# Reordering the candidate rows of a recurrent step and moving part of its operand preparation to GpSimd

## The chip, the cores and the metric

The kernel runs on one core of one Trainium2 chip. The metric is device time in microseconds (us), from one launch to its end; six runs of the kernel before gave a median of 1867.87 us (1865.36 to 1874.88). A profile of one execution goes with it. The engines of a core are named as the profile names them: PE (TensorE matrix multiply; PEld is its weight load), DVE (VectorE), ACT (ScalarE), POOL (GpSimd) and SP (SyncE, which here issues the DMAs). Each engine takes its own instructions strictly in the order in which the program has them, and waits on semaphores of others.

## The reference, cut to what matters

The input x has shape (4, 512, 512): batch B = 4, time T = 512, width D = 512. Four layers follow one another, each added to its input:

```python
x = x + attention(x, cond)               # 16 heads, RMS norm of q and k, all 512 keys
x = x + gru(cond, x)                     # one GRU over the 512 time steps
x = x + causal_conv(x, cond)             # 4 taps, depthwise
x = x + causal_conv(x, cond) + b         # 4 taps, depthwise
```

The GRU is the part that cannot be done in parallel over time. Its cell is:

```python
def cell(h, x):
    gi = x @ W_ih + b_ih
    gh = h @ W_hh + b_hh
    i_r, i_z, i_n = jnp.split(gi, 3, axis=-1)
    h_r, h_z, h_n = jnp.split(gh, 3, axis=-1)
    r = jax.nn.sigmoid(i_r + h_r)
    z = jax.nn.sigmoid(i_z + h_z)
    n = jnp.tanh(i_n + r * h_n)
    h_new = (1.0 - z) * n + z * h
    return (h_new, h_new)
```

## The kernel before, in words

A prologue of about 230 us loads and splits the weights, and computes keys, values and the first block. Then one loop over the 512 time steps runs the GRU (lines 1204 to 1272). All other work (attention, the products x @ W_ih and the convolutions, in 16 blocks of 32 time steps) is cut into small tasks that fill the gaps of the loop.

**One step of the loop.** The state h (4 batches of 512) is held as 128 partitions by 16 columns (k, b): k is one of four slices of 128 features, b the batch. It exists as an fp32 tile HS and an fp16 tile A; the kernel multiplies A by the low half of the weights (Wlo, fp16), and both A and the remainder HS - A by the high half (Whi), so that the product is good to about fp32. `prep` (line 1126) builds the operand tile BT for the next step, in eight slots of (k, b): DVE writes HS - A into slots 0 and 2 (line 1130), ACT writes A into the four odd slots (line 1131), and slots 4 and 6 stay zero. ACT also writes HH, half the state (line 1132). Then in each step

- PE adds to X (PSUM, r and z gates): 16 matmuls of A with Wlo, 16 of slots 0 and 1 of BT with Whi; and to Y (PSUM, n gate): 16 matmuls of slots 4 to 7 with Wlo and 16 of slots 0 to 3 with Whi (lines 1230 to 1239). The four column groups of PE each work on their own quarter of the features, and each quarter gives rows of 32 partitions, of which Y uses 16: slot by batch, four rows (batches) for each of four slots.
- DVE transposes X in blocks of 32 by 32 into TX (line 1241) and adds pairs into S (1243); ACT takes a tanh of it into ZT, the gates (1244).
- DVE transposes Y into TY (1253). The rows of Y come in the order slot, batch; the scan after it wants the four slots of each batch side by side, so the transposition writes with the batch innermost, at a step of four fp32 elements.
- DVE runs a scan over ZT and TY that sums the slots and multiplies by the gate (N, 1254), ACT takes the tanh (D1, 1255), DVE computes the other half of D1 from ZT and HH (1256), and two scans give the new A (1264) and HS (1265). PE waits for A and begins the next step.
- ACT also puts the next step's input products, G, into X (seedX, 1121) and Y (seedY, 1124), and POOL writes h + x into x2b for the convolutions (1269). G is loaded by SP, eight DMAs for every four steps (`load_g`, 1089), one step's four batches onto four neighbouring partitions of each group of 32.

**What sets the order.** The instruction order is fixed when the program is built. A small planner (class `Queue`) holds the tasks with priorities. Before the step's own matmuls, `q_.head` issues stages of tasks within a budget of modelled time for each engine (DVE 1130 ns, ACT 1900, POOL 3300); a single stage that costs more than the budget is let in if nothing of its engine has been issued in this step. After the step's own elementwise work, `q_.pe` issues matmuls of tasks for up to 1600 ns (2000 in the first 40 steps), and `keep_warm` adds a matmul on zeros where little was issued. Two steps before a new block of 32 steps begins (`t % 4 == GI_T`), `q_.flush` issues all that this block's input products still need, with no budget at all, ahead of the step's own matmuls. POOL's tasks are `nb` (line 447, one column, waits for DVE's row maximum `mx`), the convolution taps `tm` and `x` (lines 1168 and 1169, one pair a stage), and the Newton steps of an inverse square root for 14 of the blocks (lines 257 to 276, 13 POOL instructions, and 411 and 413; task R, line 421, one stage at a stated POOL cost of 4800).

**The end.** After the last step, the last block's convolution is issued at once: four ACT instructions (1153), then for each of six taps DVE does column groups 0 and 1 (1161), POOL groups 2 and 3; PE transposes the four groups (301), ACT copies, and SP stores.

Of the kernel before, what the change touches and what calls it, by code (L numbers as in the profile page):

```python
# [16 lines left out]
P = 128  # L17
# [145 lines left out]
def body(ctx, tc, x, cond, W_emb, b_emb, g_norm, W_qkv, g_q, g_k, W_out, W_ih, W_hh, b_ih, b_hh, L3_b, out):  # L163
# [24 lines left out]
    def rowmask(n, c):  # L188
        m = cst.tile([P, 1], F32, name=n)
        nc.vector.tensor_reduce(m, ident.rearrange("p (q s) -> p q s", q=4)[:, :, c], AX.XY, ALU.add)  # L190
        return m

    mr = mz = rowmask("mr", slice(0, 4))
    mh, mn = rowmask("mh", slice(4, 8)), rowmask("mn", slice(12, 16))

# [33 lines left out]
    BT = [cst.tile([P, 4, 8, 4], F16, name=f"BT{i}") for i in range(2)]  # L229
    for i in range(2):  # L230
        nc.gpsimd.memset(ZT[i], 1.0)
        nc.gpsimd.memset(ZT[i][:, :, :, 0:1], 0.0)
        nc.gpsimd.memset(D0[i], 0.0)
        nc.gpsimd.memset(BT[i], 0.0)
# [86 lines left out]
    def block_tasks(i):  # L321
# [72 lines left out]
        def rs0():  # L394
# [9 lines left out]
            if not pre_q:  # L404
                rsqrt(rq, v, 16, ear, nc.gpsimd)
                rs1()
# [13 lines left out]
        else:  # L420
            R = add(f"R{i}", deps=[Q], acq=["m", "L"], chunks=[(330, rch)], stages=[[("DVE", 410, rs0), ("Pool", 4800, lambda: None)]], rel=["m", "q"], settle=2)
# [638 lines left out]
    def scan_constants():  # L1060
# [4 lines left out]
        for v, m in ((sel, 1), (selY, 2)):  # L1065
            nc.gpsimd.memset(v, 0.0)
            nc.gpsimd.tensor_scalar(v[:, :, 4 * m:4 * m + 4], ident.rearrange("p (b t) -> p t b", b=4)[:, 0:2, :], 1.0, 1.0,
                                    ALU.mult, ALU.mult)

    sel, selY = lt("sel", [P, 2, 8]), lt("selY", [P, 2, 12])  # L1070
# [18 lines left out]
    def load_g(c):  # L1089
        g, i, t0_ = G[c % 2], c // 8, 4 * (c % 8)  # L1090
        for qq in range(4):
            nc.sync.dma_start(g[32 * qq + 4:32 * qq + 8, :, 0:2, :], GD[i][qq, :, t0_:t0_ + 4, 0:2, :])
            nc.sync.dma_start(g[32 * qq + 8:32 * qq + 12, :, 2, :], GD[i][qq, :, t0_:t0_ + 4, 2, :])  # L1093
# [3 lines left out]

    def dup(v):
        return v.rearrange("p (k b) -> p k b", k=4).unsqueeze(2).to_broadcast([P, 4, 2, 4])


    def seed_first(t, y):
# [12 lines left out]
        for qq in range(4 * y):  # L1115
            r = 32 * qq
            nc.tensor.matmul(Y[r:r + 12, :], selY[:, t], gs0["n"][:, qq, :], start=False, stop=True,
# [8 lines left out]
    def prep(A, HS, t):  # L1126

        Bt = BT[t % 2]
        HH = wk.tile([P, 16], F32, name="HH", tag="HH")
        nc.vector.tensor_tensor(Bt[:, :, 0:4:2, :], dup(HS[:, :, 1]), dup(A[:, :, 1]), ALU.subtract)  # L1130
        nc.scalar.activation(Bt[:, :, 1:8:2, :], A[:, :, 1].rearrange("p (k b) -> p k b", k=4).unsqueeze(2).to_broadcast([P, 4, 4, 4]), AF.Copy)  # L1131
        nc.scalar.activation(HH, HS[:, :, 1], AF.Copy, scale=0.5)
        return Bt, HH
# [11 lines left out]
    def conv_tasks(i):  # L1145
# [10 lines left out]
        def tap(k, jp):  # L1156
            def g():
                x4 = s["x4"].rearrange("p (a t) -> p a t", t=32)
                for j in (2 * jp, 2 * jp + 1):
# [139 lines left out]
```

## Time and profile before

| What | Value |
|---|---|
| median of 6 runs | 1867.87 us (1865.36 to 1874.88) |
| the profiled execution: its own time | 1867.61 us |
| its span, first to last instruction | 1865.7 us |
| PE busy | 1651.8 us, 89% |
| DVE busy | 1340.1 us, 72% |
| ACT busy | 1227.7 us, 66% |
| POOL busy | 451.6 us, 24% |
| first A of the loop to its last | 234.7 to 1846.2 us, 511 steps, 3.15 us each on average, 3.04 us median |
| after the last A | 19.5 us |
| granted TensorE clock | 0.985 |

The span is from the first to the last instruction; the execution's own time has 1.9 us around it. Busy shares are averages over stages and say little of a loop in which each engine waits for the next one: what counts in the loop is which wait ends last in a step. A line of the timeline reads: start, duration (both us), engine, source line, operation, tile written <- tiles read, and the number of instructions merged into it. A group's row ends in busy us and mean ns of one, then the engine's idle time before it and what ended it.

### The profile page before, as it was taken

The page shows a single profiled execution, that of the slowest core. Times are in us where ns is not written, and L with a number is a line of the kernel's source. Part 1 is how long each engine was busy: PE and PEld are TensorE (multiplying, and loading weights), DVE is VectorE, ACT ScalarE, POOL GpSimd, SP SyncE. Part 2 cuts the span into 40 slices and gives each one's busy share as a digit, 9 for nine tenths or more (in the row PEclk, how much of TensorE's full clock was granted, in tenths as well). Part 3 has the DMA queues.
Part 4 walks back from the last instruction along what each step waited for, and adds up shares of the span by engine and source line. Part 5 has one row for each costly group of instructions (what it writes and reads, how often), then busy time and mean ns, then how long its engine had stood idle before and what let it go on. Part 6 is the DMA issues. An engine that isn't in the chain of part 4 may idle for free.

```text
span 1865.7 us, 114008 instructions
## 1 busy us (share of the span) xinstructions
PE 1651.8 (89%) x48969; PEld 1174.9 (63%) x48969; DVE 1340.1 (72%) x4948; ACT 1227.7 (66%) x4701; POOL 451.6 (24%) x1480
## 2 busy tenths in 40 slices
PE   5789999999999999999999999999999998987553
PEld 2444567677667667676767676766667676765442
DVE  4785377776778687878777777777787877776664
ACT  4663375776767777767676767676767767665443
POOL 1255011322213131312222221313131312121212
PEclk9998899999999999999999999999999999999998
DMA  5662020101010102010101020100101010101000
GB/s 177 224 203 114 13 61 22 47 23 28 21 32 19 34 16 59 12 41 13 39 13 40 12 57 19 28 24 18 35 11 40 13 35 11 35 13 34 11 16 10
DMA packets 68921, 78.11 MB, mean 42 GB/s; under 512 B 6560, under 2 KB 54720, under 8 KB 67776
## 3 DMA queue, kind: packets, MB, share of 16 engines
q1 hardware_dynamic: 68416, 70.82, 12.6%
q8 instruction: 385, 6.31, 1.4%
q14 instruction: 120, 0.98, 0.2%
HBM read 44.58 MB, written 26.21 MB: 38 GB/s over the span
## 4 chain that ended last, share of the span: by engine, by line
PE 48%; DVE 25%; ACT 10%; DMA 6%; issue 6%; SPq 3%; POOL 1%; DVEq 0%; ACTq 0%; POOLq 0%
PE X L1227 21%; DVE TX L1241 5%; PE ps L439 5%; PE pgi L568 5%; PE Y L1227 5%; DVE TY L1253 5%; DMA G<-GD 5%; DVE N L1254 4%; PE ptp L301 4%; ACT D L1255 3%; DVE A L1264 3%; PE pkv L927 2%; PE po L483 2%; ACT X L1121 2%; SPq L1093 2%
## 5 line engine op out<-in xcount | busy, mean ns | idle before, releaser
L1227 PEld LDWEIGHTS <-BT 128*8 128x8 f16 (+1 forms) x24576 | 451.3, 88 | 81.6 <-issue 18.5
L1227 PE MATMUL X<-Wlo,A 128*4 128x256 f16 x8192 | 313.1, 272 | 125.4 <-DVE A L1264 89.1
L1244 ACT ACTIVATE ZT<-S 128x32 f32<-128x32 f32 x512 | 134.7, 263 | 415.7 <-DVE S L1243 415.1
L1269 POOL TENSOR_TENSOR x2b<-x,HS 128x16 f32<-128x16 f32 x512 | 126.8, 248 | 1130.0 <-DVE HS L1265 1128.7
L1241 DVE STREAM_TRANSPOSE TX<-X 128x256 f32<-128x256 f32 x512 | 229.4, 448 | 209.9 <-PE X L1227 208.5
L1227 PE MATMUL X<-Whi,BT 128*8 128x256 f16 x8192 | 315.7, 273 | 2.8 <-issue 2.6
L1227 PEld LDWEIGHTS <-A 128*4 128x4 f16 x8192 | 152.1, 83 | 217.6 <-DVE A L1264 191.6
L1253 DVE STREAM_TRANSPOSE TY<-Y 128x128 f32<-128x128 f32 x512 | 205.2, 401 | 10.6 <-PE Y L1227 4.3
L1227 PE MATMUL Y<-Whi,BT 128*16 128x128 f16 x8192 | 208.6, 219 | 4.7 <-issue 4.5
L1227 PE MATMUL Y<-Wlo,BT 128*16 128x128 f16 x8192 | 207.7, 219 | 4.4 <-issue 4.3
L1121 ACT ACTIVATE X<-G 128x256 f32<-128x256 f32 x510 | 202.3, 397 | 1.1 <-DMA G<-GD 0.4
L455 ACT ACTIVATE PX<-ps,nb,rqs 128x512 f32<-128x512 f32 x256 | 195.1, 762 | 8.7 <-POOL nb L447 4.7
L1254 DVE TENSOR_TENSOR_SCAN N<-ZT,TY 128x64 f32<-128x64 f32 x512 | 153.3, 299 | 54.7 <-ACT ZT L1244 2.1
L446 DVE TENSOR_REDUCE mx<-ps 128x1 f32<-128x512 f32 x256 | 174.8, 683 | 15.5 <-PE ps L439 15.4
L1264 DVE TENSOR_TENSOR_SCAN A<-D,D 128x32 f16<-128x32 f32 x512 | 115.3, 225 | 93.9 <-ACT D L1255 91.4
L301 PE MATMUL ptp<-ident,PX 128*128 128x128 f32 x1024 | 173.3, 291 | 1.0 <-ACT gs L576 0.6
L1131 ACT ACTIVATE BT<-A 128x64 f16<-128x64 f16 x512 | 131.2, 256 | 52.7 <-DVE A L1264 4.1
L301 PEld LDWEIGHTS ptp<-ident,PX 128*128 128x128 f32 x1024 | 111.4, 143 | 81.8 <-issue 43.7
L475 ACT ACTIVATE PT<-ptp 128x512 f32<-128x512 f32 x248 | 143.3, 582 | 15.1 <-PE ptp L301 15.1
L1124 ACT ACTIVATE Y<-G 128x128 f32<-128x128 f32 x510 | 141.5, 277 | 0.5 <-DMA G<-GD 0.5
L483 PEld LDWEIGHTS po<-V,PT 128*32 128x32 f32 x8192 | 99.0, 112 | 60.7 <-issue 51.8
L483 PE MATMUL po<-V,PT 128*32 128x32 f32 x8192 | 130.7, 200 | 5.8 <-issue 4.8
(266 smaller groups left out, 2806.6 us busy)
## 6 DMA issues: line engine op xcount, KB each, us to landing
GD<-gs SPq DMA_DIRECT2D x45, 256.0 KB
G<-GD SPq DMA_DIRECT2D x512, 16.0 KB
G<-GD SPq DMA_DIRECT2D x512, 8.0 KB
xp<-in_x_dram SPq DMA_DIRECT2D x16, 256.0 KB
xb<-in_x_dram SPq DMA_DIRECT2D x16, 256.0 KB
xhl<-XD SPq DMA_DIRECT2D x32, 128.0 KB
out_dram<-ob SPq DMA_DIRECT2D x16, 256.0 KB
wst<-in_L_cond_W_qkv_dram SPq DMA_DIRECT2D x6, 512.0 KB
```

The lines of the kernel that those rows point to most:

```text
L301: nc.tensor.transpose(dst[:, 128 * j:128 * j + 128], src[:, 128 * j:128 * j + 128], ident)
L446: nc.vector.tensor_reduce(s["mx"][:, h:h + 1], s[("s", j, q)], AX.X, ALU.max)
L455: nc.scalar.activation(pe_, s[("s", j, q)], AF.Exp, bias=s["nb"][:, h:h + 1], scale=s["rqs"][:, h:h + 1], accum_out=s["ls"][:, h:h + 1])
L475: nc.scalar.activation(pt_, s[("pt", h)], AF.Copy)
L483: nc.tensor.matmul(s["po"][32 * b:32 * b + 32, 32 * h:32 * h + 32], s["PT"][h][:, kt, 32 * b:32 * b + 32], V[:, 4 * b + kt, 32 * h:32 * h ...
L1121: nc.scalar.activation(X.rearrange("p (g c) -> p g c", g=2), G[(t // 4) % 2][:, t % 4, 0:2, :], AF.Copy)
L1124: nc.scalar.activation(Y, G[(t // 4) % 2][:, t % 4, 2, :], AF.Copy)
L1227: nc.tensor.matmul(dst[32 * qq:32 * qq + M, :], lhs, W[:, k, cols].rearrange("p g (j q s) -> p q g j s", j=4, q=4)[:, qq], start=False, st ...
L1241: nc.vector.transpose(TX.rearrange("p a r -> p (a r)"), X)
L1253: nc.vector.transpose(TY.rearrange("p h j b k -> p j h k b"), Y.rearrange("p (j h k b) -> p j h k b", j=4, h=2, k=4))
L1254: nc.vector.tensor_tensor_scan(f(NN), f(zt[:, 0]), TY[:, 0].rearrange("p j b k -> p (j b k)"), 0.0, ALU.mult, ALU.add)
L1264: nc.vector.tensor_tensor_scan(f(An), f(d0), f(D1), 0.0, ALU.mult, ALU.add)
```

## The change

Six things change together.

1. BT becomes two tiles. BX (k, 2 slots, b) serves X: DVE writes HS - A into slot 0 (16 columns instead of 32), ACT copies A into slot 1. BY (k, b, 4 slots) serves Y, with the slots innermost: POOL writes HS - A into slots 1 and 2, ACT copies A into slots 0 and 3. The low weights' 16 matmuls for Y now read all of BY too, so no zero slots remain and the rows of both products agree.
2. The rows of Y are so ordered by batch and then slot. The transposition into TY writes runs of 16 neighbouring elements. The seeds of Y, the masks for the biases and the DMAs into G follow: a G load for the n gate now goes to four partitions that lie four apart.
3. HH is computed by POOL, after BY and before x2b.
4. Task R has two stages, of stated POOL costs 1300 and 2000. The first issues the Newton steps up to the square of the second iteration, the second the rest and `rs1`.
5. In the last block, POOL keeps only column group 3, and DVE takes group 2 as well as 0 and 1.
6. The two memsets of BT go.

In the changed program's instruction order, the loop's waits follow: PE's first weight load from BX waits for DVE and ACT, the first from BY for ACT and POOL; DVE's part of D1 waits for POOL (HH); POOL's write of BY waits for DVE and PE.

```diff
@@ -188 +188 @@
-    def rowmask(n, c):
+    def rowmask(n, sel):
@@ -190 +190 @@
-        nc.vector.tensor_reduce(m, ident.rearrange("p (q s) -> p q s", q=4)[:, :, c], AX.XY, ALU.add)
+        nc.vector.tensor_reduce(m, sel(ident.rearrange("p (q b s) -> p q b s", q=4, b=8)), AX.XY, ALU.add)
@@ -193,2 +193,2 @@
-    mr = mz = rowmask("mr", slice(0, 4))
-    mh, mn = rowmask("mh", slice(4, 8)), rowmask("mn", slice(12, 16))
+    mr = mz = rowmask("mr", lambda v: v[:, :, 0, :])
+    mh, mn = rowmask("mh", lambda v: v[:, :, 0:4, 1]), rowmask("mn", lambda v: v[:, :, 0:4, 3])
@@ -229 +229,2 @@
-    BT = [cst.tile([P, 4, 8, 4], F16, name=f"BT{i}") for i in range(2)]
+    BX = [cst.tile([P, 4, 2, 4], F16, name=f"BX{i}") for i in range(2)]
+    BY = [cst.tile([P, 4, 4, 4], F16, name=f"BY{i}") for i in range(2)]
@@ -234 +234,0 @@
-        nc.gpsimd.memset(BT[i], 0.0)
@@ -405,2 +405,8 @@
-                rsqrt(rq, v, 16, ear, nc.gpsimd)
-                rs1()
+                s["nw"] = rsqrt_ops(rq, v, 16, ear, nc.gpsimd)
+                for _ in range(6):
+                    next(s["nw"])
+        def rs2():
+            for _ in s["nw"]:
+                pass
+            rs1()
@@ -421 +427 @@
-            R = add(f"R{i}", deps=[Q], acq=["m", "L"], chunks=[(330, rch)], stages=[[("DVE", 410, rs0), ("Pool", 4800, lambda: None)]], rel=["m", "q"], settle=2)
+            R = add(f"R{i}", deps=[Q], acq=["m", "L"], chunks=[(330, rch)], stages=[[("DVE", 410, rs0), ("Pool", 1300, lambda: None)], [("Pool", 2000, rs2)]], rel=["m", "q"], settle=1)
@@ -1065 +1071 @@
-        for v, m in ((sel, 1), (selY, 2)):
+        for v, c in ((sel, slice(4, 8)), (selY, slice(2, 16, 4))):
@@ -1067 +1073 @@
-            nc.gpsimd.tensor_scalar(v[:, :, 4 * m:4 * m + 4], ident.rearrange("p (b t) -> p t b", b=4)[:, 0:2, :], 1.0, 1.0,
+            nc.gpsimd.tensor_scalar(v[:, :, c], ident.rearrange("p (b t) -> p t b", b=4)[:, 0:2, :], 1.0, 1.0,
@@ -1070 +1076 @@
-    sel, selY = lt("sel", [P, 2, 8]), lt("selY", [P, 2, 12])
+    sel, selY = lt("sel", [P, 2, 8]), lt("selY", [P, 2, 16])
@@ -1093 +1099 @@
-            nc.sync.dma_start(g[32 * qq + 8:32 * qq + 12, :, 2, :], GD[i][qq, :, t0_:t0_ + 4, 2, :])
+            nc.sync.dma_start(g[32 * qq + 2:32 * qq + 18:4, :, 2, :], GD[i][qq, :, t0_:t0_ + 4, 2, :])
@@ -1097,4 +1102,0 @@
-    def dup(v):
-        return v.rearrange("p (k b) -> p k b", k=4).unsqueeze(2).to_broadcast([P, 4, 2, 4])
@@ -1117 +1119 @@
-            nc.tensor.matmul(Y[r:r + 12, :], selY[:, t], gs0["n"][:, qq, :], start=False, stop=True,
+            nc.tensor.matmul(Y[r:r + 16, :], selY[:, t], gs0["n"][:, qq, :], start=False, stop=True,
@@ -1128 +1130,7 @@
-        Bt = BT[t % 2]
+        Bx, By = BX[t % 2], BY[t % 2].rearrange("p k b s -> p (k b) s")
+        h4, a4 = (v[:, :, 1].rearrange("p (k b) -> p k b", k=4) for v in (HS, A))
+        two = lambda v: v[:, :, 1].unsqueeze(2).to_broadcast([P, 16, 2])
+        nc.vector.tensor_tensor(Bx[:, :, 0], h4, a4, ALU.subtract)
+        nc.gpsimd.tensor_tensor(By[:, :, 1:3], two(HS), two(A), ALU.subtract)
+        nc.scalar.activation(Bx[:, :, 1], a4, AF.Copy)
+        nc.scalar.activation(By[:, :, 0:4:3], two(A), AF.Copy)
@@ -1130,4 +1138,2 @@
-        nc.vector.tensor_tensor(Bt[:, :, 0:4:2, :], dup(HS[:, :, 1]), dup(A[:, :, 1]), ALU.subtract)
-        nc.scalar.activation(Bt[:, :, 1:8:2, :], A[:, :, 1].rearrange("p (k b) -> p k b", k=4).unsqueeze(2).to_broadcast([P, 4, 4, 4]), AF.Copy)
-        nc.scalar.activation(HH, HS[:, :, 1], AF.Copy, scale=0.5)
-        return Bt, HH
+        nc.gpsimd.tensor_scalar(HH, HS[:, :, 1], 0.5, 1.0, ALU.mult, ALU.mult)
+        return Bx, BY[t % 2], HH
@@ -1156 +1162 @@
-        def tap(k, jp):
+        def tap(k, jp, js=None):
@@ -1159 +1165 @@
-                for j in (2 * jp, 2 * jp + 1):
+                for j in js or (2 * jp, 2 * jp + 1):
@@ -1173,2 +1179,3 @@
-                  stages=[[("ACT", 700, lambda jp=jp: f1(jp))] for jp in range(2)] + [
-                      [("Pool", 900, tap_p(k, j))] + ([("DVE", 526, tap(k, 0))] if j == 2 else []) for k in range(1, 7) for j in (2, 3)],
+                  stages=[[("ACT", 700, lambda jp=jp: f1(jp))] for jp in range(2)] + ([
+                      [("Pool", 900, tap_p(k, j))] + ([("DVE", 526, tap(k, 0))] if j == 2 else []) for k in range(1, 7) for j in (2, 3)] if i < NB - 1 else [
+                      [("Pool", 900, tap_p(k, 3)), ("DVE", 526, tap(k, 0)), ("DVE", 300, tap(k, 1, (2,)))] for k in range(1, 7)]),
@@ -1202 +1209 @@
-        Bt, HH = prep(A, HS, 0)
+        Bx, By, HH = prep(A, HS, 0)
@@ -1233 +1240 @@
-                mm(X, Bt[:, k, 0:2, :].rearrange("p s b -> p (s b)"), 8, Whi, k, slice(0, 2))
+                mm(X, Bx[:, k].rearrange("p s b -> p (s b)"), 8, Whi, k, slice(0, 2))
@@ -1237 +1244 @@
-                mm(Y, Bt[:, k, 4:8].rearrange("p s b -> p (s b)"), 16, Wlo, k, slice(2, 3))
+                mm(Y, By[:, k].rearrange("p b s -> p (b s)"), 16, Wlo, k, slice(2, 3))
@@ -1239 +1246 @@
-                mm(Y, Bt[:, k, 0:4].rearrange("p s b -> p (s b)"), 16, Whi, k, slice(2, 3))
+                mm(Y, By[:, k].rearrange("p b s -> p (b s)"), 16, Whi, k, slice(2, 3))
@@ -1253 +1260 @@
-            nc.vector.transpose(TY.rearrange("p h j b k -> p j h k b"), Y.rearrange("p (j h k b) -> p j h k b", j=4, h=2, k=4))
+            nc.vector.transpose(TY.rearrange("p h j b k -> p j h (b k)"), Y.rearrange("p (j h r) -> p j h r", j=4, h=2))
@@ -1268 +1275 @@
-                Bt, HH = prep(A, HS, t + 1)
+                Bx, By, HH = prep(A, HS, t + 1)
```

## The prediction

> **What bounds the kernel now.** I read the page's chain of waits first, then the groups by line, then the timeline of single steps, and last the windows around the longest step.
>
> ```profile
> span 1865.7 us, 114008 instructions
> ...
> PE 48%; DVE 25%; ACT 10%; DMA 6%; issue 6%; SPq 3%; POOL 1%; DVEq 0%; ACTq 0%; POOLq 0%
> ...
> L1253 DVE STREAM_TRANSPOSE TY<-Y 128x128 f32<-128x128 f32 x512 | 205.2, 401 | 10.6 <-PE Y L1227 4.3
> ```
>
> No engine bounds the loop alone: the chain runs through PE, DVE and ACT in turn. One plain step, and the end of the step before it, in the timeline:
>
> ```profile
> 589.62 0.61 DVE L1161 SCALAR_TENSOR_TENSOR x<-x2b,VC,x 128x128 f32<-128x128 f32 x2
> 589.78 0.60 POOL L1168 TENSOR_SCALAR tm<-x2b,VC 128x128 f32<-128x128 f32 x1
> ...
> 592.39 0.22 DVE L1264 TENSOR_TENSOR_SCAN A<-D,D 128x32 f16<-128x32 f32 x1 [0.18 <-ACT D L1255]
> 592.53 0.20 DVE L1265 TENSOR_TENSOR_SCAN HS<-D,D 128x32 f32<-128x32 f32 x1
> ...
> 592.76 0.19 DVE L1130 TENSOR_TENSOR BT<-HS,A 128x32 f16<-128x32 f32 x1
> 592.81 0.25 POOL L1269 TENSOR_TENSOR x2b<-x,HS 128x16 f32<-128x16 f32 x1 [1.71 <-DVE HS L1265]
> ...
> 593.03 0.37 POOL L1168 TENSOR_SCALAR tm<-x2b,VC 128x128 f32<-128x128 f32 x1
> ...
> 593.48 0.46 POOL L1169 TENSOR_TENSOR x<-tm,x 128x128 f32<-128x128 f32 x1
> 593.54 0.40 PE L1227 MATMUL Y<-Wlo,BT 128*16 128x128 f16 x16
> ...
> 593.76 0.45 DVE L1241 STREAM_TRANSPOSE TX<-X 128x256 f32<-128x256 f32 x1 [0.21 <-PE X L1227]
> ...
> 594.25 0.19 DVE L1243 TENSOR_TENSOR S<-TX 128x32 f32<-128x32 f32 x1
> ...
> 594.36 0.40 DVE L1253 STREAM_TRANSPOSE TY<-Y 128x128 f32<-128x128 f32 x1
> 594.47 0.27 ACT L1244 ACTIVATE ZT<-S 128x32 f32<-128x32 f32 x1 [0.70 <-DVE S L1243]
> ...
> 594.86 0.30 DVE L1254 TENSOR_TENSOR_SCAN N<-ZT,TY 128x64 f32<-128x64 f32 x1
> 594.94 0.21 ACT L1247 ACTIVATE D<-ZT 128x16 f32<-128x16 f32 x1
> ...
> 595.19 0.18 ACT L1255 ACTIVATE D<-N 128x16 f32<-128x16 f32 x1
> ...
> 595.41 0.23 DVE L1264 TENSOR_TENSOR_SCAN A<-D,D 128x32 f16<-128x32 f32 x1 [0.18 <-ACT D L1255]
> ```
>
> The step is 3.02 us from A to A. PE starts 0.28 after A and its Y matmuls at 1.15; then TX, S, TY, N, the tanh D and A follow without a hole. N starts 0.10 after TY's end and 0.12 after ZT's. Over the 512 steps the first is 103 ns (102 to 104 in most), the second 124 ns in the median. In the 14 steps where ZT came late, N started 32 ns after ZT. So TY holds N, and ZT would hold it about 92 ns earlier.
>
> A second bound stands beside this chain: PE's filler. In 112 of 511 steps PE's first X matmul starts more than 60 ns after A's end (55 is the least): PE was still at other work.
>
> **The change, part by part.** Moments below count from a step's start at A. The sum is made against the profiled execution, 1867.61 us, 0.26 under the median.
>
> *TY (once a step).* A transposition of the same size, also from PSUM, that writes its columns in order:
>
> ```profile
> L397 DVE STREAM_TRANSPOSE rt<-pr x16: 305/308/310, 62.7 to 1489.9; 128x128 f32<-128x128 f32 x16
> ```
>
> TY takes 401 and steps four elements per write; the new one writes runs of 16. I take 308, so 93 ns less (bounds: 0, if a pattern of several dimensions is what costs, and 93). Next late is ZT, which allows 92, and then ACT: the tanh D follows the ACT instruction before it (L1247) by at least 119 ns, and here by 250, so it allows 130 in this step. Taking the least of the three in every step gives a mean of 79 ns. A step whose PE had no slack gains nothing, one with little slack gains that: summed over 511 steps this is 26 (by matmul durations) to 30 us (by PE's idle time before X). I take -27, bounds -22 to -30 where TY falls as said.
>
> *prep on DVE and ACT.* DVE's 32 columns (195 ns, L1130) become 16 (164, from the 16-column row L1256): 30 ns earlier for the filler behind it. ACT's 256 + 202 ns become two copies, near 202 each: HH leaves, and the filler behind starts no later. PE's first weight load from BX is wanted at 0.69 and BX is there by 0.57: 0.
>
> *BY on POOL (512 instructions).* It starts where x2b starts, 0.42, and costs between 0.25 (x2b, 16 columns) and 0.46 (L1169, 128 columns); 0.27 by the nearer row. It lands at 0.67 to 0.88, and PE's Y matmuls start at 1.15: 0. Behind it on POOL stand HH (0.20) and x2b, so all other POOL work begins 0.43 later. HH lands by 0.9, or 1.2 behind DVE's taps, against its reader at 2.65: 0. `nb` feeds an exponential of the next step: 0. PE gains a double wait at BY's first weight, with Y and the filler queued behind it: today's double wait between X's Wlo and Whi matmuls costs nothing (0.43 us from start to start, and 0.44 from Whi to Y, where nothing waits), so 0. BY's own wait for PE's reading two steps back is long met; D1's for HH has the scans A and HS behind it.
>
> The page "GPSIMD Engine Reference" of the Trainium skill, section Engine selection, speaks against this move: elementwise work with two inputs runs about half as fast there. By that rule an estimate for BY is 2 x 195 = 390 ns, landing at 0.81, still early, and the sum stays.
>
> *Meetings of DVE and POOL.* The first two lines of the timeline fence show one: beside DVE's two taps POOL's `tm` took 0.60, alone 0.37. The other way round, in 8 steps BT met POOL's `x` and took 338 ns instead of 192, ending 46 ns after it. With POOL 0.43 later, `x` reaches to 1.98 in a step without DVE taps (S runs 1.86 to 2.06 there: 46 ns after `x` is 2.03, so 0, up to 0.06 if BY is slower, in about 90 steps). In a step with DVE taps and `mx`, S runs 2.09 to 2.28 and `x` to 2.30, so S ends 0.06 later: 66 steps, +4 us. I take +5, bounds 0 and 12.
>
> The page "SBUF — State Buffer" of the Trainium skill, section Who interferes with whom, calls this an exclusive lock and would let each such pair wait out the other. The rows agree for `x` and the taps, not for x2b: it overlapped BT in every step and both kept their times. By the rule BY would begin only when DVE's subtraction ends, at 0.54, and land by 1.0, still ahead of 1.15.
>
> *Newton stages.* One POOL instruction follows another by 0.29 (steps after 595.4). The second stage has 9 behind x2b: to 1.11 + 2.65 = 3.76, where the next BY wants POOL at 3.37. That BY lands 0.4 late, near 1.10, against 1.15. 14 blocks: 0 to 1.4 us, I take 0.5.
>
> *What the planner makes of the new POOL costs.* 4800 shut POOL to all other tasks for a step, 1300 and 2000 do not, so tasks shift. In the program order of the changed kernel DVE's taps meet `mx` in 66 steps instead of 49: 17 x 0.23 (the step at 589.14 is 3.25 long against 3.02), less 30 ns of BX in some 70 late steps: +2 us (0 to 4). More weighty: before, one flush falls into the loop, at step 62:
>
> ```profile
> 434.50:443.40 8.90, 8.86 (x245) 7.08 (x244) 3.15 (x10) 4.35 (x15) 0.44 (x2) 1.00 0.17 45
> ```
>
> The columns are stretch, length, then busy time of PE, PEld, DVE, ACT and POOL. A to A it is 8.87, thus 5.85 more than a plain step, and PE is busy throughout. The changed order has that flush and two more, ahead of steps 190 and 350, with 35 `pgi`, 20 `ps`, 10 `ptp` and 48 `po` matmuls each, the same PE time within 5%. 2 x 5.85 = +11.7 (9 to 14). The work so brought forward no longer overfills other steps: -3.7, from PE time by step in both orders.
>
> *The G loads.* As many DMAs of the same size on SP's queue, to partitions four apart: their landing is not shown. They are issued three steps, 9 us, ahead of use, and ACT now waits 0.5 us for them in all: 0; a loss would need that cover gone.
>
> *The end.*
>
> ```profile
> 1846.58 5.21 DVE L1161 SCALAR_TENSOR_TENSOR x<-x2b,VC,x 128x128 f32<-128x128 f32 x12
> ...
> 1857.42 0.45 POOL L1169 TENSOR_TENSOR x<-tm,x 128x128 f32<-128x128 f32 x1
> ```
>
> POOL's 12 pairs, 0.92 each, end at 1857.87. Six end near 1852.4; DVE's 18 taps, 0.43 beside POOL and about 0.27 alone, end near 1853.5 and are last. -4 us (-3.3 to -4.4). Memsets and masks of the prologue: beside DMA waits, 0.
>
> Sum: -27 - 3.7 + 11.7 + 2 + 5 + 0.5 - 4 = -15.5, so 1852 for the profiled execution, 1852.4 against the median. With all ends at their best 1839, at their worst 1870.
>
> **The rivals.** (B) Slower: the shorter TY does not move N, because ZT's release costs as much as TY's does now (0.10 instead of 0.03), or TY stays at 401. For it: N has two waits, and the 32 ns come from 14 steps alone. Against it: those steps agree with every other release from ACT to DVE (D to A, 32 ns). With N unmoved the 27 are gone: 1880. With ZT at 0.10 the mean shift is 28 ns, worth 11: 1869. It decides the sign when the loop gains less than 11.5, about 34 ns a step. (C) Meetings and flushes cost their upper bounds, POOL's later queue holding S: 1853 + 7 + 2.3 = 1862. For it: POOL's busy time nearly doubles, 452 us by 512 x 0.47 more. (D) Flushes half absorbed (+6), no meetings, the loop gains 30: -30 - 3.7 + 6 + 2 - 4 = 1838. For it: steps after a flush are emptier.
>
> **How the numbers follow.** The forecast 0.50 (own range 1843 to 1861), D 0.24, C 0.13, B 0.13. No change means within 0.2%, 1864.1 to 1871.6, about what a measurement of this kernel can tell. The forecast and D are faster, of C half, of B one third falls within 0.2%: faster 0.80, same 0.11, slower 0.09. Range: 1836 to 1870; it leaves out B's slow end and some of D.
>
> **What would show it.** TY at 308 to 320 ns; N still 0.10 after TY, or 0.03 after ZT; plain steps near 2.94; BY at 0.42 and ended by 0.9, PE's Y still at 1.15; HH ahead of D1's reader; two new steps of 8.5 to 9 us near the 190th and 350th; POOL's last `x` near 1852 less what the loop gained. Wrong would be: TY over 380; PE's Y matmuls released by POOL; S or Bx stretched by POOL in more than a hundred steps; flush steps over 10 us.

## The result, and the profile after

The changed kernel takes 1871.79 us (median of 37 runs, 1857.55 to 1880.5); the kernel before, beside it, 1869.35 (79 runs, 1858.62 to 1880.96). The ratio is 1.0006 with a 95% interval of 0.9994 to 1.0017: no difference that can be measured. Forecast were 1852 and 0.80 for faster. The profiled execution took 1877.26 us.

From the page of the changed kernel: the span, the chain by engine, and the groups of ACT's seed and of TY.

```profile
span 1875.5 us, 116044 instructions
...
PE 46%; DVE 17%; ACT 13%; issue 5%; DMA 2%; SPq 1%; POOL 0%; ACTq 0%; DVEq 0%; POOLq 0%
...
L1123 ACT ACTIVATE X<-G 128x256 f32<-128x256 f32 x510 | 201.4, 395 | 10.3 <-DMA G<-GD 8.4
...
L1260 DVE STREAM_TRANSPOSE TY<-Y 128x128 f32<-128x128 f32 x512 | 158.2, 309 | 14.4 <-PE Y L1234 8.6
```

TY fell from 401 to 309 ns, as forecast. DVE's share of the chain went from 25 to 17%. New are ACT's waits for DMAs into G, 8.4 us ahead of X's seed; before, they were 0.4. One plain step in the timeline of the changed kernel:

```profile
827.77 0.22 DVE L1271 TENSOR_TENSOR_SCAN A<-D,D 128x32 f16<-128x32 f32 x1 [0.18 <-ACT D L1262]
...
828.15 0.18 DVE L1133 TENSOR_TENSOR BX<-HS,A 128x16 f16<-128x16 f32 x1
...
828.26 0.25 POOL L1134 TENSOR_TENSOR BY<-HS,A 128x32 f16<-128x32 f32 x1 [0.59 <-DVE HS L1272]
...
828.47 0.21 POOL L1138 TENSOR_SCALAR HH<-HS 128x16 f32<-128x16 f32 x1
...
828.92 0.40 PE L1234 MATMUL Y<-Wlo,BY 128*16 128x128 f16 x16
...
829.74 0.31 DVE L1260 STREAM_TRANSPOSE TY<-Y 128x128 f32<-128x128 f32 x1
...
829.86 0.26 ACT L1251 ACTIVATE ZT<-S 128x32 f32<-128x32 f32 x1 [1.48 <-DVE S L1250]
...
830.15 0.30 DVE L1261 TENSOR_TENSOR_SCAN N<-ZT,TY 128x64 f32<-128x64 f32 x1
...
830.71 0.26 DVE L1271 TENSOR_TENSOR_SCAN A<-D,D 128x32 f16<-128x32 f32 x1 [0.18 <-ACT D L1262]
```

The step is 2.94 us against 3.02. BY starts 0.49 after A and ends at 0.74; PE's Y matmuls still start at 1.15; N starts 0.10 after TY's end and 0.03 after ZT's. So the plain step does what the prediction said. Yet from the first A to the last the loop takes 1614.3 us (245.4 to 1859.7), before 1611.5. Here is one flush step of the changed kernel, the one ahead of step 190, and the step after it, by windows (stretch, length, busy time of PE, PEld, DVE, ACT, POOL, granted clock, DMA):

```profile
851.69:861.76 10.07, 9.41 (x232) 6.70 (x230) 3.23 (x11) 5.00 (x15) 1.00 (x5) 1.00 0.20 56
861.76:866.49 4.73, 3.44 (x115) 2.32 (x113) 2.35 (x9) 2.61 (x11) 0.81 (x4) 1.00 0.11 28
```

The flush step is 10.07 us long, not 8.9 (flush steps of over 10 us were one of the prediction's signs of being wrong), and the step behind it is long too: PE is busy for only 3.44 of its 4.73 us.

The end, after the last A at 1859.74:

```profile
1860.12 7.25 DVE L1167 SCALAR_TENSOR_TENSOR x<-x2b,VC,x 128x128 f32<-128x128 f32 x18
...
1865.98 0.45 POOL L1175 TENSOR_TENSOR x<-tm,x 128x128 f32<-128x128 f32 x1
```

DVE is last now, at 1867.37; from the last A to the end it is 15.8 us, before 19.5.

The span itself also holds 10.7 us of the prologue that are not the change's. The same 65 us of the prologue, before and then after, by windows (PEclk is third from the right):

```profile
170.00:235.00 65.00, 59.07 (x1159) 36.10 (x1166) 26.52 (x61) 26.63 (x65) 4.63 (x23) 0.84 0.23 89
```

```profile
170.00:235.00 65.00, 60.52 (x980) 35.14 (x979) 24.34 (x53) 24.99 (x59) 6.09 (x27) 0.61 0.20 81
```

The clock granted there was 0.61 instead of 0.84. Over the profiled executions of all kernels here, it was 0.61 to 0.89, and the first A lies anywhere from 231.1 to 246.9. Loops are therefore compared from first to last A, and kernels by the ratio of their times to the kernel before on the same chip.

### The profile page after: what moved, and what is told of

Same layout as the page of the kernel before. It is cut to its first block, busy times and chain, and to the rows that moved or that the text cites. A ratio compares the mean times of both kernels' runs of the same rounds, so it can differ in the third digit from the quotient of the medians.

```text
span 1875.5 us, 116044 instructions
## 1 busy us (share of the span) xinstructions
PE 1653.9 (88%) x48977; PEld 1186.6 (63%) x48977; DVE 1288.3 (69%) x4954; ACT 1188.7 (63%) x4701; POOL 635.9 (34%) x2490
## 4 chain that ended last, share of the span: by engine, by line
PE 46%; DVE 17%; ACT 13%; issue 5%; DMA 2%; SPq 1%; POOL 0%; ACTq 0%; DVEq 0%; POOLq 0%
PE X L1234 21%; PE pgi L574 6%; PE Y L1234 6%; DVE TX L1248 5%; PE ps L445 5%; ACT X L1123 4%; PE ptp L301 3%; DVE A L1271 3%; DVE S L1250 2%; ACT D L1262 2%; PE po L489 2%; DVE x L1167 2%; ACT D L1254 1%; DVE N L1261 1%; ACT PX L461 1%
## 5 line engine op out<-in xcount | busy, mean ns | idle before, releaser
L1134 POOL TENSOR_TENSOR BY<-HS,A 128x32 f16<-128x32 f32 x512 | 127.5, 249 | 1008.6 <-DVE HS L1272 943.5
L1234 PE MATMUL X<-Whi,BX 128*8 128x256 f16 x8192 | 316.1, 273 | 2.0 <-issue 1.8
L1234 PEld LDWEIGHTS <-BY 128*16 128x16 f16 x16384 | 277.7, 90 | 30.7 <-issue 18.5
L1234 PE MATMUL Y<-Whi,BY 128*16 128x128 f16 x8192 | 210.0, 219 | 7.3 <-issue 7.2
L1234 PE MATMUL Y<-Wlo,BY 128*16 128x128 f16 x8192 | 210.0, 219 | 5.8 <-issue 4.2
L1234 PEld LDWEIGHTS <-BX 128*8 128x8 f16 x8192 | 186.2, 86 | 43.7 <-issue 4.2
L301 PE MATMUL ptp<-ident,PX 128*128 128x128 f32 x1024 | 179.4, 296 | 1.8 <-issue 0.9
L1260 DVE STREAM_TRANSPOSE TY<-Y 128x128 f32<-128x128 f32 x512 | 158.2, 309 | 14.4 <-PE Y L1234 8.6
L1135 ACT ACTIVATE BX<-A 128x16 f16<-128x16 f16 x512 | 110.8, 216 | 53.8 <-DVE A L1271 2.1
```

Of the source, the lines that this page charges most:

```text
L301: nc.tensor.transpose(dst[:, 128 * j:128 * j + 128], src[:, 128 * j:128 * j + 128], ident)
L1234: nc.tensor.matmul(dst[32 * qq:32 * qq + M, :], lhs, W[:, k, cols].rearrange("p g (j q s) -> p q g j s", j=4, q=4)[:, qq], start=False, st ...
L1260: nc.vector.transpose(TY.rearrange("p h j b k -> p j h (b k)"), Y.rearrange("p (j h r) -> p j h r", j=4, h=2))
```

## The experiments

Words that the expectations use. *The changed kernel's* loop has, by my theory **G**, really gained from TY, and gives it back in the two extra flushes and in G's later landing. Rival **P**: POOL's part of `prep` gives it back. Rival **F**: PE's filler bounds the loop, so nothing of TY reaches the end.

**1. The stages of R, and the order of G's loads.** Four edits: R back in one stage; the split of R alone in the kernel before; and, in the changed kernel with either form of R, the four loads of the r and z rows ahead of the four of the n rows:

```diff
-            R = add(f"R{i}", ..., stages=[[("DVE", 410, rs0), ("Pool", 1300, lambda: None)], [("Pool", 2000, rs2)]], rel=["m", "q"], settle=1)
+            R = add(f"R{i}", ..., stages=[[("DVE", 410, rs0), ("Pool", 4800, lambda: None)]], rel=["m", "q"], settle=2)
```

```diff
             nc.sync.dma_start(g[32 * qq + 4:32 * qq + 8, :, 0:2, :], GD[i][qq, :, t0_:t0_ + 4, 0:2, :])
+        for qq in range(4):
             nc.sync.dma_start(g[32 * qq + 2:32 * qq + 18:4, :, 2, :], GD[i][qq, :, t0_:t0_ + 4, 2, :])
```

> The changed kernel with the Newton steps of R in one stage again (planner cost 4800, settle 2); everything else of the change stays. In program order the two extra flushes ahead of steps 190 and 350 are gone, and DVE's taps meet mx in 49 steps instead of 66. Theory G (the shorter TY does shorten the loop, and it is given back by the two flushes and by the later landing of G): in the trace of the changed kernel each flush step with the step after it is about 8.9 us longer than two plain steps, so 17 to 20 us are gained over the changed kernel, some 1853 us against 1870 before (ratio 0.989 to 0.992). Theory P (POOL's part of prep, its queue and its meetings with DVE take it back): POOL's instructions per step are the same here, so within 4 us of the changed kernel, ratio 0.998 to 1.002. Theory F (PE's filler bounds the loop, so that no ns of TY reaches the end): PE has the same work, so within 4 us of the changed kernel as well.

> The kernel before with the split of R into two stages alone (planner costs 1300 and 2000, settle 1). In program order it has flushes ahead of steps 62, 190 and 350. Theory G: two flush steps of 9 to 10 us in place of plain ones, with the steps after them 17 us longer, less 2 to 4 us of other steps: +13 to +18 us, ratio 1.007 to 1.010. By the price that the prediction took (5.85 each, less 3.7) it would be +8. Theories P and F: nothing of POOL's prep is here and PE's work is the same: within 3 us, ratio 0.998 to 1.002.

> The changed kernel with the eight loads of G issued in another order: the four of the r and z rows (L1098) first, then the four of the n rows (L1099). In the trace of the changed kernel SP spends 459 ns on one of the former and 631 ns on one of the latter (before: 299 and 299), so the last of the former is issued 1.9 us earlier here. Theory G: ACT's waits on G's DMAs (8.4 us in the changed kernel, 0.4 before) fall to 2 us or less and the time by 5 to 9 us against the changed kernel, ratio to before 0.996 to 0.998. If the n rows are what is waited for, nothing changes. Theories P and F: within 3 us of the changed kernel.

> The changed kernel with both edits: R in one stage, and the loads of the r and z rows first. Theory G: both gains, 22 to 28 us under the changed kernel, ratio to before 0.985 to 0.989; what is left of TY's gain in the loop is then 25 us or more. Theories P and F: within 5 us of the changed kernel, ratio 0.997 to 1.003.

| Kernel | ratio | interval |
|---|---|---|
| a_oneR | 1.0032 | 1.0010 to 1.0054 |
| b_splitR | 1.0108 | 1.0080 to 1.0135 |
| a_xfirst | 0.9937 | 0.9914 to 0.9960 |
| a_oneR_xfirst | 1.0026 | 1.0002 to 1.0049 |

G was right in sign on the split (20 us for the flushes in the kernel before, where 13 to 18 were expected) and on the loads (13 us, where 5 to 9 were), and wrong on R in one stage: no gain at all, and 1 us for the loads there, where ACT waits 4.0 us for G instead of 8.4. One row of PE's waits in a_oneR says why (us in total, times, longest):

```profile
PE Y L1228 <- POOL BY L1128: 20.9, 13, 1.8
```

Undivided, the Newton steps stand on POOL ahead of the next BY, and PE waits for it. In the changed kernel this row is 0.2 us. So the split pays on POOL about what its flushes cost; a_oneR did not test the flushes alone.

**2. POOL out of `prep`, Newton steps in two parts, G's partitions.** Theory **H** is G with the Newton wait added. a_noPool_xfirst has BY's subtraction on DVE and HH on ACT; a_pend_xfirst plans R in one stage but issues six Newton steps there and the rest behind x2b; a_contig loads G's n rows to neighbouring partitions and leaves Y's seeds as they are, so that they come from the wrong rows and only its time counts.

```diff
 a_noPool_xfirst (on a_oneR_xfirst)
-        nc.gpsimd.tensor_tensor(By[:, :, 1:3], two(HS), two(A), ALU.subtract)
+        nc.vector.tensor_tensor(By[:, :, 1:3], two(HS), two(A), ALU.subtract)
-        nc.gpsimd.tensor_scalar(HH, HS[:, :, 1], 0.5, 1.0, ALU.mult, ALU.mult)
+        nc.scalar.activation(HH, HS[:, :, 1], AF.Copy, scale=0.5)
 a_pend_xfirst (on a_oneR_xfirst)
-                rsqrt(rq, v, 16, ear, nc.gpsimd)
-                rs1()
+                s["nw"] = rsqrt_ops(rq, v, 16, ear, nc.gpsimd)
+                for _ in range(6):
+                    next(s["nw"])
+                PEND.append(rs2)     # issued behind x2b of the same step
 a_contig (on the changed kernel)
-            nc.sync.dma_start(g[32 * qq + 2:32 * qq + 18:4, :, 2, :], GD[i][qq, :, t0_:t0_ + 4, 2, :])
+            nc.sync.dma_start(g[32 * qq + 8:32 * qq + 12, :, 2, :], GD[i][qq, :, t0_:t0_ + 4, 2, :])
```

> The changed kernel with R in one stage, the loads of the r and z rows first, BY's subtraction on DVE and HH on ACT: what is left of the change is the order of Y's rows with the shorter TY, the two operand tiles and the last block's taps. Theory H (after the first four runs: TY's 92 ns are worth some 28 us; the two flushes took 19 of them, the later landing of G some 13; with R in one stage BY waits on POOL behind the Newton steps, 20.9 us in 13 steps): nothing of that is left here, so -28 of TY and -4 of the end, +0 to +8 for DVE's longer queue: ratio to before 0.983 to 0.987. Theory F (PE's filler bounds the loop): ratio 0.995 or more.

> The changed kernel with the loads of the r and z rows first, and R planned in one stage (4800, settle 2, so no extra flush), but its Newton steps emitted in two parts: six when R runs, the rest behind x2b of the same step, so that BY stands between them. BY's subtraction and HH stay on POOL. Theory H: PE's wait for BY (22.0 us in 14 steps with one part) goes, the flushes at steps 190 and 350 do not come: ratio to before 0.984 to 0.990, within 5 us of the kernel without POOL in prep. Theory P (POOL's part of prep costs time of itself, by meetings with DVE and by its queue): this one is 8 us or more slower than the kernel without POOL in prep.

> The changed kernel with G's n rows loaded to four neighbouring partitions instead of partitions four apart, in the old order of the eight loads; the seeds of Y then come from the wrong rows, everything else is computed as in the changed kernel. If the partitions four apart are what makes SP slow (631 ns for one such issue, and 459 for the r and z rows between them): both kinds are back near 299 ns, ACT's waits on G fall from 8.4 us to 1 or less, and the time is that of the kernel with the r and z rows first, ratio 0.992 to 0.996. If the two extra flushes or POOL's queue hold SP back instead: 0.6 us stay, and the time stays within 3 us of the changed kernel.

> The changed kernel itself, on the same chip as the three others. Every theory: ratio 0.999 to 1.002. It gives its rows beside theirs: by theory H PE waits under 1 us for BY in all, ACT 7 to 10 us for G, and the steps 62, 190 and 350 last 9.9 to 10.4 us each.

| Kernel | ratio | interval |
|---|---|---|
| a_noPool_xfirst | 0.9935 | 0.9913 to 0.9958 |
| a_pend_xfirst | 0.9938 | 0.9915 to 0.9961 |
| a_contig | 0.9921 | 0.9890 to 0.9952 |
| after_again | 0.9994 | 0.9968 to 1.0020 |

*G's loads.* SP's issues by line, in the kernel before and in the changed one (ns, least/median/most; the first line of each pair loads the r and z rows):

```profile
L1092 SPq DMA_DIRECT2D G<-GD x512: 241/299/1153, 234.0 to 1820.5; - x171
L1093 SPq DMA_DIRECT2D G<-GD x512: 241/299/1157, 234.7 to 1820.8; - x171
```

```profile
L1098 SPq DMA_DIRECT2D G<-GD x512: 240/459/1249, 244.9 to 1836.2; - x171
L1099 SPq DMA_DIRECT2D G<-GD x512: 624/631/842, 245.6 to 1836.7; - x171
```

The same issues in the timeline of the changed kernel, then of a_contig, which differs in nothing else:

```profile
820.08 0.62 SPq L1099 DMA_DIRECT2D G<-GD  x1
820.75 0.46 SPq L1098 DMA_DIRECT2D G<-GD  x1
821.25 0.62 SPq L1099 DMA_DIRECT2D G<-GD  x1
```

```profile
563.41 0.24 SPq L1099 DMA_DIRECT2D G<-GD  x1
563.70 0.29 SPq L1098 DMA_DIRECT2D G<-GD  x1
564.04 0.29 SPq L1099 DMA_DIRECT2D G<-GD  x1
```

The median is 631 ns for an n load to partitions four apart and 459 for the r and z loads between them; before, and in a_contig, 299 for each. A set of eight holds SP's queue 4.64 us instead of 2.87. ACT's waits for G fall with it, from 8.4 us in the changed kernel to these in a_contig:

```profile
ACT X L1123 <- DMA G<-GD: 1.2, 3, 0.8
```

With the r and z loads first they are 0.5 for X and 1.4 for Y, although SP still takes 608 ns for an n load. The late steps of the changed kernel were the 1st, 31st, 63rd, 191st, 319th and 351st (4.1 to 6.2 us each); in a_xfirst they are together 9.4 us shorter, and in a_contig 8.7 shorter than in after_again. Three of the six stand directly behind a flush. a_xfirst and a_contig are 10 to 16 us under the changed kernel, by which of its ratios is taken: the cost is the pattern of these DMAs in the order that they had. Some 9 us of it are seen in the six steps; the rest is not tied to any step.

*H is not confirmed in size.* Without flushes, G's wait and POOL's part, TY and the end give 12 us together where H had 24 to 32. F, that nothing of TY reaches the end, is not borne out, though not yet excluded: 0.9935, and 0.9940 when repeated in study 4, lie under its 0.995, but their intervals reach it. (Beside the flushes of study 4 the same edits are worth 21 us, which excludes it.) a_noPool_xfirst and a_pend_xfirst are equal, which speaks against P; in the latter PE still waits 4.9 us for BY behind the first six Newton steps. A loss of 12 to 20 us was left, which the next two studies look for.

**3. PE's instruction fetches.** The profile puts a wait down to "issue" when it shows nothing that the engine waited for. In the traces such waits of PE are higher in kernels with the short TY than in those with the long one and the same flushes. One of them, in a_noPool_again, of PE's timeline:

```profile
831.55 0.61 PE L1229 MATMUL X<-Wlo,A 128*4 128x256 f16 x16 [0.24 <-DVE A L1266]
831.99 0.28 PE L1229 MATMUL X<-Whi,BX 128*8 128x256 f16 x4
833.23 0.50 PE L1229 MATMUL X<-Whi,BX 128*8 128x256 f16 x12 [0.95 <-issue]
```

PE stops for 0.95 us between the fourth and the fifth matmul of one group, whose operand was complete. A DMA packet started between 830.4 and 830.5 us in this kernel; the DMA view of that window gives its queue, the number of packets, MB and share:

```profile
q8 instruction: 1, 0.02, 73.2%
```

It landed at 831.65, and PE resumes 1.58 us later. The page of the kernel before has this row for the queue:

```profile
q8 instruction: 385, 6.31, 1.4%
```

These are packets of 16 KB, and the kernel has 97,938 PE instructions (matmuls and weight loads): 254 for each. In the ten profiles so far (before, after, studies 1 and 2) PE has 394 such stalls of over 150 ns in the loop, 7.2 to 26.7 us a profile. All 394 end 1.1 to 1.75 us after a packet of this queue has landed; the packets start mostly 3.4 to 6.0 us apart, so of stalls with no tie to them about one in six would. Theory **I**: PE uses up a packet's instructions before the next is there. Rival **W**: the stalls belong to the instructions where they stand. The test adds 64, 128 or 192 PE instructions at the start of a_pend_xfirst, in a wait of the prologue, so that the packets' edges fall elsewhere in an unchanged loop:

```diff
     clear()
+    for _ in range(32):          # 64 and 96 in the other two
+        nc.tensor.matmul(idle[:, 0:4], zz[:, 0:128], zz[:, 0:4], start=False, stop=True, skip_group_check=True)
```

> The kernel a_pend_xfirst again, as the base of the three that follow, on their chip. Ratio 0.991 to 0.996; PE's stalls that the profile puts down to issue come to 15 to 25 us between 260 and 1820 us (22.8 in its first profile), in much the same steps as there (the 96th, 128th, 187th, 192nd, 256th, 352nd and others).

> a_pend_xfirst with 32 more matmuls of 4 columns (64 PE instructions with their weight loads) at the very start of the program, while PE waits 14 to 15 us for its first DMA; the loop is the same. Theory I (PE runs dry at the edges of its instruction fetches: the page lists some 386 packets of 16 KB on the instruction queue, and 43 of the 44 stalls put down to issue end 1.1 to 1.6 us after such a packet landed): the edges now fall 64 PE instructions earlier in the program, so the stalls are at other steps, their sum is another one (anything from 7 to 27 us, the span seen over the runs so far), and the time moves with the sum: 1 us of issue stalls is 0.6 to 1 us of time. Rival W (the stalls belong to the instructions where they stand, waits that the profile does not show): the same steps stall, and the time is within 2 us.

> The same with 64 matmuls, 128 PE instructions. Theory I: other steps again, another sum; over the four of this series the spread of the sums is 5 us or more and that of the times follows it. Rival W: the same steps, within 2 us.

> The same with 96 matmuls, 192 PE instructions. Theory I and rival W as for the two before; by theory I the best of the four is 3 us or more under their mean.

| Kernel | ratio, interval | issue stalls of PE, 260 to 1820 us | steps shared with a_pend_again | mean time at clock 0.98 |
|---|---|---|---|---|
| a_pend_again | 0.9969 (0.9947 to 0.9992) | 33.1 us, 62 | | 1863.2 us |
| a_pend_shift64 | 0.9925 (0.9892 to 0.9959) | 27.7 us, 55 | 27 | 1859.0 us |
| a_pend_shift128 | 0.9950 (0.9927 to 0.9974) | 28.0 us, 58 | 19 | 1859.3 us |
| a_pend_shift192 | 0.9946 (0.9923 to 0.9969) | 31.9 us, 64 | 32 | 1862.4 us |

The last column takes out the granted clock: all kernels lose 12.2 us for 0.01 of mean clock, fitted over all runs with 2.2 us left over. The unshifted kernel's two profiles share 36 stalling steps of 44; a shift leaves 19 to 32. The times follow the stalls, some 0.75 us for one. a_pend_again itself lies above both of its bounds, 0.996 and 25 us. I is supported and W refuted, though not cleanly: expected were a spread of 5 us in both and a best 3 us under the mean; the spreads are 5.4 and 4.2, the best 2 under the mean. The sum also differs between chips: the same kernel had 22.8 us on another one, where a packet took 1084 ns instead of 1123.

**4. Flush by TY, on one chip.** What the flushes cost with the long and with the short TY, and what PE's fetches cost in each. a_noPool_again is a_noPool_xfirst once more, and a_noPool_split is a_xfirst with the two edits that take POOL out. Theory **M**: a loop in which PE's work ends last gets part of the flush back.

> The kernel before itself, for its trace on the chip of the three others. Every theory: ratio 1, TY 401 ns. By theory I (PE runs dry at the edges of its instruction fetches) PE's stalls put down to issue come to 10 to 20 us between 260 and 1820 us here, against 20 us or more in the kernel with the shorter TY and no extra flush.

> The kernel before with R in two stages: long TY, two more flushes. Its first measurement was 1.0108. Theory M (a chain bound by TX, S, TY and A cannot use the PE work that a flush brings forward): 1.007 to 1.011 again.

> Short TY, no POOL in prep, R in one stage, no extra flush. Its first measurement was 0.9935. Every theory: 0.991 to 0.996. Against the kernel before on this chip, by theory I: issue stalls 6 us or more higher.

> Short TY, no POOL in prep, R in two stages, so two more flushes. If the price of the flushes adds to the rest (18.8 us in the kernel before): ratio 1.002 to 1.006. Theory M: with the shorter TY more steps end with PE's filler, and PE work brought forward by a flush shortens those: the flushes cost 8 us or less, ratio 0.990 to 0.998, and PE's issue stalls are 5 us or more under those of the kernel without the flushes.

| | no extra flush | two more flushes |
|---|---|---|
| long TY | 1 (before_again: issue stalls 14.0 us) | 1.0097, 1.0066 to 1.0128 (11.9 us) |
| short TY, no POOL | 0.9940, 0.9910 to 0.9970 (28.7 us) | 0.9984, 0.9963 to 1.0004 (21.7 us) |

PE's waits between 260 and 1820 us (us in total, times, longest), in before_again and in a_noPool_again:

```profile
PE X L1227 <- ACT Y L1124: 26.8, 52, 1.3
PE Y L1227 <- issue: 7.4, 16, 1.0
PE po L483 <- issue: 3.5, 5, 1.8
PE X L1227 <- issue: 2.9, 8, 0.7
```

```profile
PE po L483 <- issue: 10.3, 15, 2.4
PE Y L1229 <- issue: 9.2, 21, 0.8
PE X L1229 <- issue: 8.4, 19, 1.0
```

The issue rows are what grew. The shorter step asks for as many PE instructions in less time, and PE runs dry 14.7 us more. (ACT's seed of Y, the first row, held PE's X in 52 steps; with the short TY that row is 4.4 us.) The flushes cost 18 us with the long TY and 8 with the short one, where 7 us of the stalls go; that their work relieves other steps is concluded from the difference. M's sign holds, but each price is uncertain by some 6 or 7 us; M's price of 8 or less is met on the line, the ratio of 0.9984 is just above the bound that was set, and in study 5 the same kernel came to 1.0004 on another chip. Read by columns, the table says that the short TY with its layout and the end is worth 11 us without the flushes and 21 us beside them.

From first to last A the loop of a_noPool_again is 9.6 us shorter than that of before_again. The plain step gives 86 ns, 44 us in 511 steps. Summing by step how much later each link of the chain starts than in a plain step, the rest goes: PE's first X matmul after A +15.8 us, the X matmuls +7.2, TX behind DVE's other work +5.7, the start of N +5.0, its tanh +3.7; the link from there to A gives some 3 us back.

**5. POOL's part of `prep`, side by side.** a_xfirst and a_noPool_split differ in the two edits of study 2 alone.

> The changed kernel with the loads of the r and z rows first (BY's subtraction and HH on POOL), on one chip with the next. Ratio 0.991 to 0.997 (0.9937 at first). If POOL's part of prep is worth something of itself: 5 to 12 us faster than the next one, with TX waiting 8 us or more less for DVE's other work over the loop. If the difference between their first measurements (0.9937 and 0.9984) came from the chips: within 4 us of it.

> The same with BY's subtraction on DVE and HH on ACT. Ratio 0.996 to 1.001 (0.9984 at first) if POOL's part is worth 5 to 12 us, 0.992 to 0.997 if it is worth nothing.

a_xfirst_again came to 0.9941 (0.9914 to 0.9967), a_noPool_split_again to 1.0004 (0.9979 to 1.0028). DVE's idle time ahead of TX, in the one and in the other:

```profile
DVE TX L1249 <- PE X L1235: 237.5, 422, 2.2
```

```profile
DVE TX L1249 <- PE X L1235: 163.2, 255, 1.9
```

With BY on POOL, DVE waits for X in 422 steps; with BY on DVE (236 ns) in 255, since its own filler ends later. The lateness of TX sums to 17.4 us against 29.6. So beside the flushes POOL's part is a gain of 12 us, at the upper end of what was expected. Without them no gain is seen: a_pend_xfirst, with BY on POOL, and a_noPool_xfirst were equal, the former with 4.9 us of waits for BY behind the Newton steps. Both results of a_xfirst lie under the kernel before and the changed one, as do the two of a_noPool_xfirst (0.9935 and 0.9940).

## Why the prediction was wrong

The changed kernel taken apart by the runs, each part as a difference of ratios times 1867 us, beside the term of the sum:

| Term | Predicted | Measured | From |
|---|---|---|---|
| short TY in the loop | -27 | -8 | a_noPool_xfirst and a_noPool_again, less the end |
| flushes and what they relieve, taps, second Newton stage | +10.5 | +11 | a_noPool_split less a_noPool, both times |
| POOL's part of prep: BY, HH, meetings | +5 | -12 | a_xfirst_again less a_noPool_split_again |
| G's loads | 0 | +11 | the changed kernel less a_xfirst, both times |
| the end | -4 | -3.7 | the two traces |
| sum | -15.5 | -2 | the change itself: +1 (-1 to +3) |

Each measured row is the step from one kernel to the next, so the rows add up to the change by construction; the 3 us left over are repeats on other chips, and a row is uncertain by some 5 us. The order of the steps decides how the first three rows share their sum. With the flushes first, in the kernel before, they cost 19 us (b_splitR, both times); the short TY beside them then gives 17 (a_noPool_split less b_splitR_again, less the end) and POOL's part 12. In either order the three come to -9 or -10, where the prediction had -11.5.

**The step that failed** is therefore the term that it put at nothing: "They are issued three steps, 9 us, ahead of use, and ACT now waits 0.5 us for them in all: 0". G's loads cost 10 to 13 us by a_xfirst. With nothing but their order changed, the kernel is 11 to 12 us under the kernel before, at 1856 to 1857 us, within the forecast's own range. That the other terms hold in sum is in part luck, since three of them were mis-sized and their errors cancel.

- *TY.* Its duration, what holds N, ZT as next and the plain step all came out as written. The term of -27 was too large: -8 without the flushes, -17 beside them. Both rows hold DVE's second subtraction (236 ns a step) too; no run has the short TY without it and without BY on POOL. The sum "over 511 steps" let PE's slack cap the gain step by step, with PE's program taking as long as in the trace of before. The cap itself is not far off (a mean of 79 ns is 40 us, capped to 27; X late +15.8, some of it fetches). Not in it was that PE gets its instructions no faster in a shorter step, 14.7 us of issue stalls more, some 11 us at the 0.75 of study 3. The trace before already had the row: 15.6 us of PE waits put down to issue.
- *The flushes.* With the short TY the net is near, 8 and 13 us, by two errors that cancel. Each is 7.0 us over a plain step instead of 5.85 (9.9 to 10.5 long in the split kernels, and the old one at step 62 went from 8.9 to 9.7 and more), and what they relieve is, by difference, 1 to 6 us rather than 3.7. With the long TY the same sum would have been 8 to 10 us too low: the price of a flush depends on the kernel around it, by theory M on whether the chain or PE ends the steps there.
- *POOL.* BY a little after 0.42 (0.51 in the median), landing at 0.75, HH ahead of its reader, PE's Y at 1.15: right. S and its meetings cost 2.3 us in place of 4. What failed is "30 ns earlier for the filler behind it": costed for the kernel before, where BT takes 195 ns, when the layout alone would give DVE two subtractions, 175 and 236 ns. Against that layout the move to POOL is a gain of 12 us beside the flushes.
- *G's loads.* The cover of 9 us was counted per DMA; the eight share SP's queue, which another pattern made 1.8 us longer, and at the first steps and behind a flush there was no cover. The prediction said itself that their landing was not shown, and yet gave the term neither a bound nor a place in the range: no trace of before has a DMA to partitions apart.
- *Newton.* That the second stage is free held (0.2 us of PE waiting for BY). That the first form would not have been, 20.9 us, the prediction did not say.
- *The end.* Right: -3.7 against -4.
- *The rivals.* The sums of B and C start from 1853, 1 us above the prediction's own. B's mechanism did not occur: N followed ZT by 31 to 40 ns in 458 steps. Of C, whose 1862 is nearer, the flushes did cost their upper bound (14 us for two), but POOL's later queue did not hold S (2.3 us) and its part gains. POOL's busy time went from 452 to 636 us; the 241 us that C adds would not nearly have doubled it either. None of the rivals held what happened: SP's queue, and PE short of instructions.
- *The two pages.* By "GPSIMD Engine Reference" of the Trainium skill, section Engine selection, two-input work would be half as fast on POOL: BY takes 249 ns there and 236 on DVE. The lock of "SBUF — State Buffer", section Who interferes with whom, does not show for these two: BY began at 828.26 while DVE's BX ran from 828.15 to 828.33. BX took 175 ns in the median with BY on POOL and with BY on DVE; BY took 249 in the 17 steps in which it began after BX's end, and 248 in the others.

What stays open: how much of the 10 to 13 us of G's loads is more than the 9 seen in the six late steps; how much of the 15.8 us at X belongs to PE's filler and how much to its fetches (the stalls fall into several links); and why the unchanged PE program of the changed kernel has 20.6 us of stalls in after_again and 14.5 in a_contig on the same chip.

## What to carry to other kernels

When one link of a chain of engines gets shorter, look in the trace of before at who will be asked for more per microsecond: the idle rows put down to "issue", and the instructions of the densest engine per step, not its busy time alone. Cost a moved DMA as a place in its queue, with the time that the queue is held by all its neighbours, and look for the steps where its cover is gone. Price a batch of work moved forward (a flush) by what ends the steps around it: the same two flushes cost 18 to 20 us in the kernel with the long TY and 8 to 13 in the one with the short TY.

## What the runs showed of the hardware

- A DMA of 8 KB to four partitions that lie four apart holds SP for 608 to 631 ns, to four neighbouring ones 299. The 16 KB loads issued between them went from 299 to 459, and back to 300 when issued together.
- PE's instructions come in packets of 16 KB, about one for 254 instructions, which took 1022 to 1129 ns each in the mean of a profile; PE went on 1.1 to 1.7 us after the landing. From a packet's start to the end of the stall it is 2.4 to 2.7 us in the medians, and the next one starts 1.1 to 1.3 us later: some 3.6 us for 254 instructions when PE runs dry, which is 207 in the 2.94 us of a plain step, while a step has 186 on average and over 230 in 71 to 81 of 511 steps. The Trainium skill, "Runtime: NRT & Kernel Launch", section Instruction fetch mechanics, calls the crossing of a 16 KB boundary mostly hidden; here it cost PE 7 to 33 us of a run. "Advanced Engine Details and Errata", section ISA Cache, has 16 KB lines of 256 instructions, which agrees.
- A column order of runs of 16 instead of single elements at a step of 16 bytes makes the 128x128 transposition from PSUM 309 ns instead of 401.
- The clock granted between 170 and 235 us was 0.61 in two executions of the changed kernel, 0.84 and 0.68 in two of the kernel before; over all profiles it was 0.61 to 0.89, and the loop began between 231.1 and 246.9 us.
